# Near score tiles of a relative-position attention: one product kept from the row-maximum scan instead of two, with the row maximum taken off on ScalarE

## The chip, the cores and the metric

The kernel is one program on one NeuronCore of one Trainium2 chip. The time is device time in microseconds (us) of one execution, from launch to end on the core. A core has five instruction streams that run side by side and meet through semaphores: TensorE (PE; its weight loads, PEld, are a row of their own), VectorE (DVE), ScalarE (ACT), GpSimd (POOL) and SyncE (SP), the last mostly issuing DMAs. TensorE writes its products to PSUM, which here is eight banks of 128 partitions x 512 float32 numbers.

## The reference, cut to what matters

Two layers over x of shape (B, T, D) = (2, 1024, 128). Each computes, from one layer norm, an attention and a mixture of experts side by side, and adds both to x:

```
x = x + attention0(layernorm(x)) + experts0(layernorm(x))   # sigmoid attention, 32 experts of which 4 count
x = x + attention1(layernorm(x)) + experts1(layernorm(x))   # below;             16 experts of which 4 count
```

The change lies in the second attention and, in a small part, in the sorting for the second layer's experts. The second attention has 16 heads of 8 numbers and relative positions that are clipped at 128 on either side:

```
att_rel_pos = einsum('bhsd,pd->bhsp', q, pos_emb_k)          # 256 positions
att_idxs    = clip(key - query, -128, 127) % 256
att_pos     = att_rel_pos[:, :, query, att_idxs]
att         = softmax((q @ k^T + att_pos) / sqrt(8))          # over all 1024 keys, not causal
y           = (att @ v) @ Wproj^T
```

So only keys within 128 of the query have a position term that differs from key to key. Keys farther to the left all have the one term of position -128, keys farther to the right that of 127. In experts1, each of the 2048 tokens takes 4 of 16 experts; tokens are sorted by expert into blocks of 128 rows, moved there, run through their expert's three matrices, and moved back.

## The kernel before, in words

Stages, by the time of the profiled execution: up to 519 us the first layer's attention with its experts; 519 to 883 us the first half of the second attention; 883 to 1005 us the sorted expert blocks (experts, placed in the middle of the attention); from 1005 us the second half. The change touches the two stages of the second attention, and the last steps of the first stage, in which its pipeline is filled.

**Groups and steps.** The 16 heads are four sets s of four; the four heads of a set lie in the four bands of 32 partitions, so the four small matmuls of one operation lie in different rows of TensorE's array and partly overlap. T is cut into eight tiles of 128 and two halves q of 512. A group n = (b, s, q) is a batch, a set of heads and 512 queries: 16 groups. Each has eight steps, one for each tile kt of 128 keys: 128 steps. A pair of groups, q = 0 and q = 1 of the same heads, is the period of the work.

**Softmax in two passes.** Scores are held with keys on partitions and queries along the columns, so a row maximum can't be taken there. It is found ahead of time, from products that lie the other way round:

- by_position (L844) multiplies the queries by the 256 position vectors (less that of the far left) into four banks (L853); ACT copies them out (L857), DVE fills the third 128 columns with the last one (L859), and a DMA writes the rows to a buffer in DRAM with a row pitch W (L866). near_by (L870) reads them back with a pitch one shorter, which turns "column = relative position" into "column = key": the near tile of a query tile, [128 queries, 4 heads, 3 x 128 keys].
- scan(n, i, half) (L891) runs for query tile i of group n over four of the eight key tiles: four matmuls of 512 columns into four banks (L902). The keys kls and khs (operands, L834) carry the far-left or the far-right position already. On DVE the maxima of columns that need nothing more are plain reductions (L927). For the key tiles within one of the query tile, the near tile must be added first: one instruction adds, writes the sums to a scratch buffer, junk, and takes the maximum (L922). After the second half L930 takes the maximum over the pieces, negated, into negmax. Each of the eight scans of a group belongs to one step; they run LEAD = 10 steps ahead of the scores that need them.
- augment (L932) turns the four negmax tiles of a group (L937) and adds them to the queries as one more row (L941), called qa, against a row of ones in the keys: the product then is the score less its maximum.
- scores(n, kt) (L944) takes four banks, one for each head. A key tile within one of query tile i is "near": the near tile's part is transposed into the bank by a matmul with the identity (L953), head after head and within a head tile after tile, and the product of keys and qa (L963) is added on top of it over all 512 columns. In a group, three of the eight steps have no near tile, one has one, two have two and two have three: 11 near pairs, times four heads times 16 groups are 704 transposes. ACT takes the exponential from each bank to p (L970).
- values (L974) multiplies p by the values, one step later, into an accumulator bank (acc, L982); unload (L986, L994) takes it off after the group.

**What sets the order.** In this part PE's order is written by hand and kept: step t is scores(t), values(t - 1), scan(t + 10), with values split around the scan in some steps without near tiles; then, in two steps of a group, by_position and near_by for a later group, and in one step augment. After these come the pieces of work beside: the gate and sort1 in the early steps, later the moves of rows. The order on ACT, DVE, POOL and SP is set by the framework's scheduler from dependences and its own estimates of time, once, when the program is built; each engine then runs its list in that order.

**Banks.** Seven of the eight PSUM banks are one ring, "sm": each request takes the next one, the one given out seven requests before, and PE waits until its last reader is done. Scans, scores, position products, augment and sort1 all take from it. A step asks for eight banks (four for the scores, four for the scan), so it moves one on in the ring from step to step.

**sort1** (L535) counts, from the four choices of each token, where each token goes. Two products (L550, L551) go into one bank: rank, the number of tokens ahead in the same tile with the same expert, and in_tile, the count of each tile. in_tile is copied out, a running sum over the 16 tiles is built by 15 additions on DVE, and rank is read from the bank after these (L561).

Of the kernel before, what the change touches and what calls it, by code (L numbers as in the profile page):

```python
# [46 lines left out]
def fused_layers_kernel(ctx: ExitStack, tc: tile.TileContext, a: dict, out: bass.AP):  # L47
# [487 lines left out]
    def sort1():  # L535
# [13 lines left out]
        rank, in_tile = (ps[:, i * NTT * E1:(i + 1) * NTT * E1] for i in range(2))  # L549
        nc.tensor.matmul(rank, ahead, flat[0], start=True, stop=True)  # L550
        nc.tensor.matmul(in_tile, ones, flat[0], start=True, stop=True)  # L551
        rank, in_tile = (t.rearrange("p (t e) -> p t e", e=E1) for t in (rank, in_tile))
        nc.vector.tensor_copy(some, in_tile)
        nc.vector.memset(at[:, 0, :], 0.0)
        for t in range(1, NTT):
            if t % 8 == 1:
                yield
            nc.vector.tensor_add(at[:, t, :], at[:, t - 1, :], some[:, t - 1, :])
        nc.vector.tensor_add(n_tok, at[:, NTT - 1, :], some[:, NTT - 1, :])
        yield  # L560
        nc.vector.tensor_add(at, at, rank)  # L561
# [237 lines left out]
    def rows_of(r):  # L799
        return slice(32 * r, 32 * r + 32)  # L800
# [90 lines left out]
    def scan(n, i, half):  # L891

        b, s, q = groups[n]
        l1 = pools["l1"]
# [11 lines left out]
        if half == 0:  # L906
            maxima[n, i] = l1.tile([P, NG, 4], F32, tag="maxima", name="maxima", bufs=3), []
# [6 lines left out]
        for k0, k1, close in pieces:  # L914
            slot = len(used)
            used.append(slot)
            for r in range(NG):
                part = ps[r][:, (k0 - lo) * P:(k1 - lo) * P]
                if close:
                    junk = l1.tile([P, NEAR], F32, tag="junk", name="junk")  # L920
                    w0 = (k0 - (qt - 1)) * P
                    nc.vector.tensor_tensor_reduce(  # L922
                        junk[:, 0:(k1 - k0) * P], part, near[n, i][:, r, w0:w0 + (k1 - k0) * P],
                        1.0, -BIG, ALU.add, ALU.max, mx[:, r, slot:slot + 1],
# [3 lines left out]
        if half == 1:  # L928
            out_ = negmax[s, i].rearrange("p (r c) -> p r c", r=NG)[:, :, aux[s]]
            nc.vector.tensor_reduce(out_, mx[:, :, 0:len(used)], AX.X, ALU.max, negate=True)  # L930

# [12 lines left out]
    def scores(n, kt):  # L944
# [4 lines left out]
        close = [i for i in range(4) if abs(4 * q + i - kt) <= 1]  # L949
        for r in range(NG):  # L950
            for i in close:
                w0 = (kt - (4 * q + i) + 1) * P
                nc.tensor.matmul(  # L953
                    ps[r][:, i * P:(i + 1) * P], near[n, i][:, r, w0:w0 + P], ident,
                    is_transpose=True, start=(i == close[0]), stop=False, skip_group_check=True,
                )

        cut = min(max(kt - 1 - 4 * q, 0), 4)
# [326 lines left out]
```

## Time and profile before

| what | value |
|---|---|
| time, three runs | 1305.71, 1308.27, 1313.92 us; median 1308.27 |
| profiled execution | 1308.08 us; span from the first to the last instruction 1306.3 us |
| busy, of the span | TensorE 92%, VectorE 58%, ScalarE 48%, GpSimd 29% |
| mean granted TensorE clock | 0.966 of full speed |
| busy in 519 to 883 us (364 us) | PE 335.6, DVE 249.8, ACT 184.8, POOL 77.1 us |
| busy in 883 to 1005 us (122 us) | PE 114.7, DVE 64.6, ACT 50.6, POOL 0.0 us |
| busy in 1005 to 1306.3 us (301.3 us) | PE 278.0, DVE 184.2, ACT 155.9, POOL 145.3 us |

How to read its lines: "L953 PE MATMUL sm<-ident,near 128*128 128x128 f32 x704 | 108.4, 287 | 24.5 <-DVE maxima L927 11.3" is a group of instructions: those of line 953, matmuls into a bank "sm" from the identity and a near tile, 704 of them; they were busy for 108.4 us together, 287 ns each; before them PE stood idle for 24.5 us, of which 11.3 us were ended by DVE's maxima of line 927 (which read the bank that the transpose wanted). Matmuls overlap, so the length of one is more than the distance between two. In a timeline the first two numbers are the start and the length of a run of equal instructions in us, xN their number, and [1.41 <-PE sm L902] the idle time before the first of them with what ended it.

### The profile page before, as it was taken

Reading aid. Unit: us, or ns where it says so; the run is one execution under the profiler, and the core shown is the slowest. Engines: PE = TensorE matmul, PEld = TensorE weight load, DVE = VectorE, ACT = ScalarE, POOL = GpSimd, SP = SyncE. Lnnn points to the kernel's source line nnn. Section 1 sums busy time; section 2 is a strip of 40 time slices with the busy share of each in tenths; the row PEclk is TensorE's granted clock in tenths of the full one; section 3 lists DMA queues with packets and bytes.
Section 4 is the critical chain, followed back from the end, with each engine's and each line's share of the span. In section 5 each row is a group of like instructions: output and inputs, shape, how many; then the busy total and the mean of one; then the engine's idle time right before and its main releaser. Section 6 shows DMA issues by size and latency. Waiting matters only on the chain.

```text
span 1306.3 us, 23125 instructions
## 1 busy us (share of the span) xinstructions
PE 1197.7 (92%) x8567; PEld 566.9 (43%) x8567; DVE 759.4 (58%) x2178; ACT 625.0 (48%) x1102; POOL 378.2 (29%) x464
## 2 busy tenths in 40 slices
PE   5889999989999878899799999988999999998997
PEld 2323332333333333434344354448999444443433
DVE  7783333573322358776876756764555856666653
ACT  3634444535455342454355654543444555554463
POOL 1123243323323242001002444330000445446453
PEclk9889999989999989899899999998999999998998
DMA  6682212111111261344365644659997354663511
GB/s 181 175 229 85 59 57 57 33 33 49 41 49 41 82 217 61 126 147 145 98 194 178 201 142 161 218 185 278 293 293 228 110 171 157 208 215 115 181 47 29
DMA packets 146660, 181.77 MB, mean 139 GB/s; under 512 B 16436, under 2 KB 125236, under 8 KB 146292
## 3 DMA queue, kind: packets, MB, share of 16 engines
q1 hardware_dynamic: 142292, 171.37, 42.7%
q0 software_dynamic: 4256, 8.92, 2.4%
q8 instruction: 68, 1.11, 0.4%
q14 instruction: 44, 0.36, 0.1%
HBM read 110.81 MB, written 73.77 MB: 141 GB/s over the span
## 4 chain that ended last, share of the span: by engine, by line
PE 70%; DVE 17%; DMA 5%; ACT 4%; issue 2%; POOL 1%; SPq 0%; DVEq 0%; ACTq 0%; POOLq 0%
PE sm L963 11%; PE sm L902 9%; PE acc L982 8%; PE big L340 6%; PE sm L953 5%; PE big L449 5%; PE big L341 5%; PE acc L475 5%; PE ffn L367 4%; PE sm L704 4%; DVE junk L922 3%; PE sm L853 3%; DVE maxima L927 2%; PE sm L719 2%; DMA room<-wx 1%
## 5 line engine op out<-in xcount | busy, mean ns | idle before, releaser
L970 ACT ACTIVATE p<-sm 128x512 f32<-128x512 f32 x512 | 264.7, 607 | 234.1 <-PE sm L963 233.6
L927 DVE TENSOR_REDUCE maxima<-sm 128x1 f32<-128x512 f32 (+3 forms) x472 | 226.7, 502 | 99.2 <-PE sm L902 99.2
L455 ACT ACTIVATE at<-big 128x1024 f32<-128x1024 f32 (+1 forms) x192 | 144.9, 808 | 149.7 <-PE big L449 143.7
L922 DVE CUSTOM_DVE_ANT_0 junk<-sm,near 128x384 f32<-128x384 f32 (+2 forms) x292 | 130.3, 446 | 66.3 <-PE sm L902 66.3
L982 PE MATMUL acc<-p,vs 128*32 128x512 f32 (+1 forms) x1288 | 146.4, 524 | 0.4 <-ACT yu L994 0.4
L352 DVE SCALAR_TENSOR_TENSOR t<-big,b,sg 128x512 f32<-128x512 f32 x64 | 47.9, 749 | 158.0 <-ACT sg L351 158.0
L355 POOL TENSOR_TENSOR h<-h,cb 128x512 f32<-128x512 f32 x64 | 82.8, 1294 | 195.5 <-DVE h L353 185.3
L953 PE MATMUL sm<-ident,near 128*128 128x128 f32 x704 | 108.4, 287 | 24.5 <-DVE maxima L927 11.3
L902 PE MATMUL sm<-kls,qs 32*128 32x512 f32 (+2 forms) x776 | 107.5, 580 | 6.2 <-POOL kls L834 5.0
L963 PE MATMUL sm<-qa,kls 32*128 32x512 f32 (+3 forms) x832 | 112.9, 560 | 0.0
L630 POOL DMA_INDIRECT got<-slots_y,slot_of x64 | 65.1, 1017 | 164.6 <-ACT p L970 152.5
L953 PEld LDWEIGHTS sm<-ident,near 128*128 128x128 f32 x704 | 78.0, 143 | 79.2 <-ACT p L970 35.4
L449 PE MATMUL big<-qm,xT 32*128 32x512 f32 (+3 forms) x768 | 103.8, 555 | 1.3 <-DVE xT L249 0.6
L618 POOL DMA_INDIRECT slots_x<-xn,slot_of x64 | 62.8, 981 | 95.8 <-ACT p L970 86.3
L475 PE MATMUL acc<-at,xn 128*32 128x512 f32 (+3 forms) x768 | 84.8, 514 | 5.9 <-POOL at L460 4.0
L340 PE MATMUL big<-xT,w 128*128 128x512 f32 x128 | 74.5, 665 | 14.9 <-DVE h L353 12.5
L857 ACT COPY rel<-sm 128x512 f32<-128x512 f32 x112 | 57.5, 600 | 61.6 <-PE sm L853 61.6
L640 POOL TENSOR_SCALAR got<-got,share 128x128 f32<-128x128 f32 x64 | 41.1, 642 | 110.1 <-DMA got<-slots_y,slot_of 110.0
L367 PE MATMUL ffn<-h,w 128*128 128x512 f32 x128 | 72.8, 651 | 0.0
L982 PEld LDWEIGHTS acc<-p,vs 128*32 128x32 f32 x1288 | 26.6, 109 | 105.9 <-issue 95.4
L902 PEld LDWEIGHTS sm<-kls,qs 32*128 32x128 f32 x776 | 36.9, 186 | 81.1 <-ACT p L970 21.1
L460 POOL TENSOR_SCALAR_AFFINE_SELECT at<-at 128x512 f32<-128x512 f32 x64 | 41.5, 648 | 101.6 <-ACT at L455 101.2
(285 smaller groups left out, 1659.8 us busy)
## 6 DMA issues: line engine op xcount, KB each, us to landing
bounce<-rel SPq DMA_DIRECT2D x64, 768.0 KB
near<-bounce SPq DMA_DIRECT2D x64, 768.0 KB
cb<-cw SPq DMA_DIRECT2D x128, 128.0 KB
blockw<-wx SPq DMA_DIRECT2D x53, 304.0 KB
room<-wx SPq DMA_DIRECT2D x26, 304.0 KB
slots_x<-zeros SPq DMA_DIRECT2D x19, 256.0 KB
slots_y<-by SPq DMA_DIRECT2D x19, 256.0 KB
room<-slots_x SPq DMA_DIRECT2D x17, 256.0 KB
```

Of the source, the lines that this page charges most:

```text
L340: nc.tensor.matmul(hh[0:m, 0, :], wa, xT, start=True, stop=True)
L367: nc.tensor.matmul(y, w2m, h[0:m], start=first, stop=last and bias_mm is None)
L449: nc.tensor.matmul(halves[r // 2][:, r % 2, off:TB], xT0[b][g, kt * P:(kt + 1) * P], masked[b, s][g, q * TB + off:(q + 1) * TB], start=Tru ...
L455: nc.scalar.activation(at[:, 2 * j:2 * j + 2, off:TB], sc[:, :, off:TB], AF.Sigmoid, scale=4.0 / math.sqrt(HD))
L475: nc.tensor.matmul(y[32 * r:32 * r + 32, off:TB], xn0[b][:, kt * P + 32 * r:kt * P + 32 * r + 32], at[:, r, off:TB], start=(kt == 0), stop ...
L902: nc.tensor.matmul(ps[r][:, (k0 - lo) * P:(k1 - lo) * P], qs[g, qt * P:(qt + 1) * P], (kh if far else kl)[g, k0 * P:k1 * P], start=True, s ...
L922: nc.vector.tensor_tensor_reduce(junk[:, 0:(k1 - k0) * P], part, near[n, i][:, r, w0:w0 + (k1 - k0) * P], 1.0, -BIG, ALU.add, ALU.max, mx[ ...
L927: nc.vector.tensor_reduce(mx[:, r, slot:slot + 1], part, AX.X, ALU.max)
L953: nc.tensor.matmul(ps[r][:, i * P:(i + 1) * P], near[n, i][:, r, w0:w0 + P], ident, is_transpose=True, start=(i == close[0]), stop=False, ...
L963: nc.tensor.matmul(ps[r][:, i0 * P:i1 * P], k[g, kt * P:(kt + 1) * P], qa[n][g, i0 * P:i1 * P], start=(m == 0 and not close), stop=(m == l ...
L970: e = nc.scalar.activation(p[:, r, :], ps[r], AF.Exp)
L982: nc.tensor.matmul(y[rows_of(r), part], vs[:, kt, rows_of(r)], probs[n, kt][:, r, part], start=(kt == 0), stop=(kt == NT - 1 and part.stop ...
```

## The change

**Near tiles.** The in-place sum replaces junk: in the scan the instruction that adds the near tile and takes the maximum now writes its sums, the finished scores, back into the near tile. A new function, take_off, adds negmax to these columns on ScalarE (one activation Identity with a bias column for each head; 384 columns, or 256 for the first and last query tile). In scores, the near tiles are transposed as before, but nothing is added to them: the product with qa covers only the columns that aren't near, those left of the near tiles (c0) with khs and those right of them (c1) with kls. The transposes now run tile after tile, and within a tile head after head.

**Order of the scans.** For q = 0, a group now scans the far half of the keys (key tiles 4 to 7) for its four query tiles first, then the near half for the four (tile_of); for q = 1 the order is as before. So up to six tiles of maxima are open, and L930's counterpart runs after the half that holds the last piece (half == q). In the written order of the program take_off stands after scores(t): for heads 0 and 1 two steps after the scan that finished the tile, for heads 2 and 3 three steps after.

**sort1.** Both products are copied out of the bank at once; the running sum is built in place, and rank is added at the end from the copy.

```diff
--- before.py
+++ after.py
@@ -546,19 +546,17 @@
         yield
         nc.vector.tensor_add(some, some, chosen[3])
         ps = small()
-        rank, in_tile = (ps[:, i * NTT * E1:(i + 1) * NTT * E1] for i in range(2))
-        nc.tensor.matmul(rank, ahead, flat[0], start=True, stop=True)
-        nc.tensor.matmul(in_tile, ones, flat[0], start=True, stop=True)
-        rank, in_tile = (t.rearrange("p (t e) -> p t e", e=E1) for t in (rank, in_tile))
-        nc.vector.tensor_copy(some, in_tile)
-        nc.vector.memset(at[:, 0, :], 0.0)
+        for i, m in enumerate((ahead, ones)):
+            nc.tensor.matmul(ps[:, i * NTT * E1:(i + 1) * NTT * E1], m, flat[0], start=True, stop=True)
+        nc.vector.tensor_copy(flat[1], ps[:, 0:NTT * E1])
+        nc.vector.tensor_copy(flat[0], ps[:, NTT * E1:2 * NTT * E1])
         for t in range(1, NTT):
             if t % 8 == 1:
                 yield
-            nc.vector.tensor_add(at[:, t, :], at[:, t - 1, :], some[:, t - 1, :])
-        nc.vector.tensor_add(n_tok, at[:, NTT - 1, :], some[:, NTT - 1, :])
+            nc.vector.tensor_add(some[:, t, :], some[:, t, :], some[:, t - 1, :])
+        nc.vector.tensor_copy(n_tok, some[:, NTT - 1, :])
         yield
-        nc.vector.tensor_add(at, at, rank)
+        nc.vector.tensor_add(at[:, 1:, :], at[:, 1:, :], some[:, 0:NTT - 1, :])
         by_e = [P, E1, E1]
         nc.vector.tensor_tensor(some, spread(n_tok, NTT), filled.unsqueeze(1).to_broadcast(by_e), ALU.is_gt)
         nc.vector.tensor_reduce(n_blk, some, AX.X, ALU.add)
@@ -888,9 +886,15 @@
 
     maxima = {}
 
-    def scan(n, i, half):
+    def tile_of(n, m):
+
+
+        return (m // 2, m % 2) if groups[n][2] else (m % 4, 1 - m // 4)
+
+    def scan(n, m):
 
         b, s, q = groups[n]
+        i, half = tile_of(n, m)
         l1 = pools["l1"]
         qs, kl, kh, _ = head[b, s]
         qt = 4 * q + i
@@ -903,8 +907,8 @@
                     ps[r][:, (k0 - lo) * P:(k1 - lo) * P], qs[g, qt * P:(qt + 1) * P],
                     (kh if far else kl)[g, k0 * P:k1 * P], start=True, stop=True,
                 )
-        if half == 0:
-            maxima[n, i] = l1.tile([P, NG, 4], F32, tag="maxima", name="maxima", bufs=3), []
+        if (n, i) not in maxima:
+            maxima[n, i] = l1.tile([P, NG, 4], F32, tag="maxima", name="maxima", bufs=6), []
         mx, used = maxima[n, i]
         n0, n1 = max(lo, qt - 1), min(hi, qt + 2)
         if n0 >= n1:
@@ -917,17 +921,27 @@
             for r in range(NG):
                 part = ps[r][:, (k0 - lo) * P:(k1 - lo) * P]
                 if close:
-                    junk = l1.tile([P, NEAR], F32, tag="junk", name="junk")
+
                     w0 = (k0 - (qt - 1)) * P
+                    whole_ = near[n, i][:, r, w0:w0 + (k1 - k0) * P]
                     nc.vector.tensor_tensor_reduce(
-                        junk[:, 0:(k1 - k0) * P], part, near[n, i][:, r, w0:w0 + (k1 - k0) * P],
-                        1.0, -BIG, ALU.add, ALU.max, mx[:, r, slot:slot + 1],
+                        whole_, part, whole_, 1.0, -BIG, ALU.add, ALU.max, mx[:, r, slot:slot + 1],
                     )
                 else:
                     nc.vector.tensor_reduce(mx[:, r, slot:slot + 1], part, AX.X, ALU.max)
-        if half == 1:
+        if half == q:
             out_ = negmax[s, i].rearrange("p (r c) -> p r c", r=NG)[:, :, aux[s]]
             nc.vector.tensor_reduce(out_, mx[:, :, 0:len(used)], AX.X, ALU.max, negate=True)
+
+    def take_off(n, i, heads):
+
+        b, s, q = groups[n]
+        qt = 4 * q + i
+        w0, w1 = (max(qt - 1, 0) - (qt - 1)) * P, (min(qt + 2, NT) - (qt - 1)) * P
+        for r in heads:
+            t = near[n, i][:, r, w0:w1]
+            c = 32 * r + aux[s]
+            nc.scalar.activation(t, t, AF.Identity, bias=negmax[s, i][:, c:c + 1])
 
     def augment(n):
 
@@ -946,24 +960,23 @@
         b, s, q = groups[n]
         _, kl, kh, _ = head[b, s]
         ps = [small() for _ in range(NG)]
-        close = [i for i in range(4) if abs(4 * q + i - kt) <= 1]
-        for r in range(NG):
-            for i in close:
-                w0 = (kt - (4 * q + i) + 1) * P
+        c0, c1 = (min(max(kt + d - 4 * q, 0), 4) for d in (-1, 2))
+        for i in range(c0, c1):
+            w0 = (kt - (4 * q + i) + 1) * P
+            for r in range(NG):
                 nc.tensor.matmul(
                     ps[r][:, i * P:(i + 1) * P], near[n, i][:, r, w0:w0 + P], ident,
-                    is_transpose=True, start=(i == close[0]), stop=False, skip_group_check=True,
+                    is_transpose=True, start=True, stop=True,
                 )
 
-        cut = min(max(kt - 1 - 4 * q, 0), 4)
-        parts = [(0, cut, kh)] * (cut > 0) + [(cut, 4, kl)] * (cut < 4)
-        for m, (i0, i1, k) in enumerate(parts):
+        for i0, i1, k in ((0, c0, kh), (c1, 4, kl)):
             for r in range(NG):
-                g = rows_of(r)
-                nc.tensor.matmul(
-                    ps[r][:, i0 * P:i1 * P], k[g, kt * P:(kt + 1) * P], qa[n][g, i0 * P:i1 * P],
-                    start=(m == 0 and not close), stop=(m == len(parts) - 1), skip_group_check=True,
-                )
+                if i0 < i1:
+                    g = rows_of(r)
+                    nc.tensor.matmul(
+                        ps[r][:, i0 * P:i1 * P], k[g, kt * P:(kt + 1) * P], qa[n][g, i0 * P:i1 * P],
+                        start=True, stop=True,
+                    )
         p = pools["late"].tile([P, NG * TB], F32, tag="p", name="p", bufs=2)
         p = p.rearrange("p (r c) -> p r c", r=NG)
         for r in range(NG):
@@ -1100,7 +1113,9 @@
     at(N_ATT + 8, turned1, 1)
     at(N_ATT + 9, blocks1, 1)
     for m in range(LEAD):
-        at(N_ATT + 8 + m, scan, m // 8, m % 8 // 2, m % 2)
+        at(N_ATT + 8 + m, scan, m // 8, m % 8)
+        if 4 <= m < 8:
+            at(N_ATT + 9 + m, take_off, 0, m - 4, range(NG))
     at(N_ATT + 10, by_position, 1, 1)
     at(N_ATT + 13, queries, 0, 1)
     at(N_ATT + 13, operands, 0, 1)
@@ -1197,6 +1212,12 @@
             if t < N_STEPS:
                 scores(t // 8, t % 8)
 
+            for back in (2, 3):
+                m = t + LEAD - back
+                n, k = m // 8, m % 8
+                if LEAD - 2 <= m < N_STEPS and (k % 2 if groups[n][2] else k >= 4):
+                    take_off(n, tile_of(n, k)[0], range(2 * back - 4, 2 * back - 2))
+
 
             n, kt = (t - 1) // 8, (t - 1) % 8
             halved = 0 < kt and t != EXPERTS and t + 1 < N_STEPS and not is_near(t + 1) and not before
@@ -1204,7 +1225,7 @@
                 values(n, kt, left if halved else whole)
             m = t + LEAD
             if m < N_STEPS:
-                scan(m // 8, m % 8 // 2, m % 2)
+                scan(m // 8, m % 8)
             if halved:
                 values(n, kt, right)
             for f, args in before:
```

## The prediction

> **What bounds the kernel now.** I read the page's busy shares first, then windows by stage, then the groups by shape, then the timeline of single steps.
>
> ```profile
> PE 1197.7 (92%) x8567; PEld 566.9 (43%) x8567; DVE 759.4 (58%) x2178; ACT 625.0 (48%) x1102; POOL 378.2 (29%) x464
> ```
> ```profile
> 1056.40:1133.10 76.70, 74.14 (x657) 34.33 (x658) 51.78 (x167) 42.22 (x83) 38.81 (x53) 1.00 0.57 180
> ```
> TensorE is the busiest engine overall. The second line is one undisturbed pair of groups (16 of the 128 steps; columns: length, then busy time of PE, weight loads, DVE, ACT and POOL, clock, DMA). PE is busy 74.1 of 76.7 us, so what PE waits for decides. I call steps 0.0 to 0.7 those of the even group (q = 0) and 1.0 to 1.7 those of the odd one; the pair starts at step 0.0.
>
> ```profile
> 1123.25 1.14 PE L902 MATMUL sm<-kls,qs 32*128 32x512 f32 x8
> 1124.32 0.55 PE L953 MATMUL sm<-ident,near 128*128 128x128 f32 x3
> 1125.32 0.30 PE L953 MATMUL sm<-ident,near 128*128 128x128 f32 x1 [0.45 <-DVE maxima L922]
> 1125.55 1.14 PE L963 MATMUL sm<-qa,kls 32*128 32x512 f32 x8
> ...
> 1131.95 1.14 PE L902 MATMUL sm<-kls,qs 32*128 32x512 f32 x8
> 1133.03 1.53 PE L953 MATMUL sm<-ident,near 128*128 128x128 f32 x12
> 1134.48 1.14 PE L963 MATMUL sm<-qa,kls 32*128 32x512 f32 x8
> ```
> Step 1.3 (one near tile): scan, three transposes, then 0.45 us idle until DVE has freed the fourth bank, one transpose, product. Step 1.5 (three tiles): twelve transposes and no wait. The scan takes four of seven banks, the scores the next four: heads 0 to 2 get the banks of the previous exps 1 to 3, head 3 the first bank that DVE gives back from the scan just done. With heads outside, three tiles hide that wait behind nine transposes.
>
> ```profile
> 1124.41 0.29 DVE L927 TENSOR_REDUCE maxima<-sm 128x1 f32<-128x128 f32 x1 [1.41 <-PE sm L902]
> 1124.62 0.55 DVE L922 CUSTOM_DVE_ANT_0 junk<-sm,near 128x384 f32<-128x384 f32 x1
> 1125.09 0.08 DVE L922 DVE_READ_ACCUMULATOR2_ANT maxima<- 128x1 f32 x1
> ```
> DVE starts when the scan ends, frees a bank each 0.68 us (1124.41 to 1125.09), and with L930 has the tile's maximum 3.0 us after that start.
>
> ```profile
> L970 ACT ACTIVATE p<-sm 128x512 f32<-128x512 f32 x512 | 264.7, 607 | 234.1 <-PE sm L963 233.6
> L351 ACT ACTIVATE sg<-big,b 128x512 f32<-128x512 f32 x64 | 44.0, 687 | 49.8 <-PE big L341 49.5
> L963 PE MATMUL sm<-qa,kls 32*128 32x512 f32 x512 | 86.1, 656 | 0.0
> ```
> ACT waits for PE before its exps and not the other way round. Four exps take 2.06 us in the timeline, just what PE needs (values 1.0, scan 1.07) before it asks for their banks.
>
> ```profile
> 620.73 0.73 PE L853 MATMUL sm<-posd,qs 32*128 32x256 f32 x6 [1.36 <-DVE at L561]
> 626.73 2.07 PE L853 MATMUL sm<-posd,qs 32*128 32x256 f32 x10 [5.26 <-DVE maxima L927]
> ```
> The sort: 1.36 us are the bank held until L561, 5.26 us are DVE busy with the sort itself.
>
> **What the Trainium skill says.** "ScalarE: Activation LUTs", What ACT_TABLE_LOAD costs: an ACTIVATE with immediates takes 186 ns + 0.833 ns per column, each pointer operand adds about 93, and following ones overlap by 93. The trace agrees: 607 for 512 columns against 612, and 687 with a bias column against 705. The same page, Table sets: identity is in every set, so no table load comes in; no Identity runs in the kernel before. "PSUM — Partial Sum Buffer", Engine vs sequencer instructions: ScalarE and VectorE queues are strict FIFO. "TensorE: Matmul & The Clock Gate", What's actually happening: an idle window of about 3.4 us halves the clock; in the sort the granted clock falls to 0.63 and 0.50, after the 5.26 us wait.
>
> **The change, part by part** (per pair).
>
> (1) Product columns that go. The start-to-start distance of a product is 1.07 us for 512 columns, 0.75 for 384, 0.54 for 256, 0.33 for 128. Before, each of 16 steps costs 1.07: 17.2. After, even group 0.54, 0.33, 0.33, 0.54, 0.75, 3 x 1.07; odd 3 x 1.07, 0.75, 0.54, 0.33, 0.33, 0.54: 11.4. That is -5.7 of PE time. The 44 transposes stay.
>
> (2) Transposes with tiles outside and heads inside (scores). PE now asks for the fourth bank after three transposes in every near step, so it waits as in step 1.3, and the rest of the transposes (0.122 us each) come after the wait: four more in a 2-tile step (+0.49, against 0.53 saved), while in a 3-tile step the product starts 1.00 + 0.23 + 8 x 0.122 = 2.2 after the first transpose instead of 1.45 (+0.73, against 0.74 saved). Four steps of each kind: +4.9. (1) and (2) together leave -0.8, nearly all from the two 1-tile steps.
>
> (3) DVE order. The built order of the changed kernel has, in two scans per pair (steps 0.1 and 1.3), the sums of all four heads ahead of the plain maxima of all four, so that the first bank comes back after 2.1 us and not 0.7: +1.4 each. Step 1.4 pays it in full. At 0.1 the position products (L853) pay it, but before's own wait there (0.6 us at 1078.70, and 0.17 in 0.2) goes: net +0.6. Together +2.0. The in-place write itself is as wide as the junk write and costs nothing; DVE's maxima order over the halves moves work between steps and adds none.
>
> (4) ScalarE. 256 new activations, 192 of 384 columns and 64 of 256: 600 and 493 ns by the page (bias is a pointer), 0.51 and 0.40 back to back; some 147 us busy, so per pair 42.2 + 18 of 77 and no bound by itself. The trace bounds it from below: 0.40 and 0.29 without the bias column. What decides is the place. PE alone has its order written by hand; ACT's built order puts the first take-off of a tile not two steps after its scan but ahead of the very next step's exps, in all pairs alike: scan 0.3 before exps 0.4, 0.5 before 0.6, 1.3 before 1.4, 1.4 before 1.5, 1.5 before 1.6. ACT then stands until DVE has that scan's maximum, 3.1 us after the scan's end, and four exps wait behind it, PE's next banks behind these.
> Step 0.4: scores end 1.9 after scan 0.3; the take-off ends at 3.1 + 0.6 = 3.7; exps 1.8 late. Head 3 of the scan waits 1.05, the next scores 0.5: +1.5. Step 0.6: exps 2.0 late, and one take-off of 0.4 stands between each two of them, so the fourth ends 3.2 late; the position products need it with 0.8 in hand: +2.4. Step 1.5: exps 1.6 late: +1.1; 1.6: +0.8 at the position products; take-offs behind the rel copies in 0.1: +0.4. Sum 6.2, less what steps 1.7 and the next 0.0 give back because their bank waits overlap with it (1.2) and about 0.5 that the 0.2 us pauses of the halved steps take up: +4.5, or +2.7 with the shorter activations.
>
> (5) Sort. The bank goes at once, -1.3 at most; two copies (0.42 each) replace one copy and a memset, and the DVE run of 9.5 us ahead of the maxima gets some 2 us shorter while the same work comes later. I take -1.3.
>
> (6) Even groups scan the far half first, so the fourth tile's near sums are wanted three steps after their positions, not four. Rows leave at 668.39 and are back at 676.4 in the SP timeline: 8 us against three steps of over 4: hidden; were it not, 1 us a pair. Six maxima buffers and the missing junk cost nothing.
>
> **Sum.** Per pair -5.7 + 4.9 + 2.0 + 4.5 = +5.7. Six pairs: +34.2. The pair with the sort hides its first terms behind it: +4.5. The last pair has no scans in its last ten steps: +3.9 from steps 0.4 and 0.6, and there the columns do count (-2.9): +1.0. Sort -1.3. Together +38.4. The profiled execution took 1308.08 us (span 1306.3 and 1.8 around it), the median of the runs 1308.27: the forecast is 1346 us. With the shorter activations it is 1333, with every give-back missing 1358: its own range is 1330 to 1362.
>
> **Rivals.** A: ACT's waits are hidden, because the exps have more slack than I read; then -0.8 + 2.0 a pair stays, +9 less 1.3 and 2.9: 1313. For it: ACT idles 234 us before the exps. Against it: this idle time lies before the scores, not after them. B, the other side: the fourth bank. If it is free when PE asks (DVE frees it 0.35 us sooner than in step 1.3, since nothing else is queued), waits (2) to (4) shrink and the columns count: -5.7 x 8 is -45, with a third of it lost to exps some -30: 1278. It decides once the bank is back within 0.6 us of the first transpose; before, it is 1.0. C: the PE pauses at L853 grow past 3.4 us, the clock halves once a pair as in the sort: 3 us more each: 1370. For it: the two waits there are over 2 us.
>
> **How the numbers follow.** Forecast 0.57, A 0.16, B 0.18, C 0.09. The range leaves out most of B and of C: 1290 to 1365. A tells from no change only by over 1% (13 us), about what this measurement can tell: slower 0.57 + 0.09 and no part of A, 0.66; within 1% 0.16; faster 0.18.
>
> **What would show it.** (1) L963's counterpart loses a third of its busy time. (2) three transposes, a pause of about 0.45 ended by DVE maxima, then the others, in 2- and 3-tile steps. (3) a pause near 1.9 in step 1.4. (4) take-offs waiting for DVE negmax, exps starting over 1.5 us after the scores' end, and a PE pause at the position products of 0.6 ended by ACT p. (5) the wait for L561 gone, 5 us on DVE maxima left. The forecast is wrong if ACT's exps still start within 0.1 us of the scores.

## The result, and the profile after

The changed kernel takes 1383.78 us (median of 4 runs, 1375.78 to 1387.33), the kernel before 1306.99 us beside it: a ratio of 1.057, 95% interval 1.0508 to 1.0632. It is slower by 77 us, where 38 were forecast (1346 us, with 1290 to 1365 as the range). The profiled execution took 1384.05 us, with a span of 1382.3 us and a mean granted clock of 0.934 (before: 0.966). Below, a run that lay over 1.5% above the fastest of its kernel is left out of ratios and means (one each of E11 and E13).

The page's busy shares come first:

```profile
PE 1236.5 (89%) x8247; PEld 578.1 (42%) x8247; DVE 754.1 (55%) x2178; ACT 745.7 (54%) x1358; POOL 377.9 (27%) x464
```

TensorE issues 320 matmuls fewer, and yet it is busy for 39 us more: its matmuls run at a lower clock. Its idle time (span less busy) grew too, from 108.6 to 145.8 us. The next lines are the two rows of PE's waits that changed most, and the row of DVE's that is new (total us, times, longest):

```profile
PE sm L851 <- DVE maxima L931: 39.5, 14, 6.1
PE sm L967 <- DVE maxima L931: 19.4, 32, 1.6
```
```profile
DVE near L927 <- DMA near<-bounce: 24.2, 7, 5.6
```

L851 are the position products (L853 before). Their wait for DVE is 39.5 us now; the same row of the trace before has 9.4:

```profile
PE sm L853 <- DVE maxima L927: 9.4, 15, 5.3
```

In 7 cases DVE itself stood still, because the near tile it was to add hadn't come back from DRAM. No such row stood in the trace of before.

The groups of ScalarE, by shape:

```profile
L983 ACT ACTIVATE p<-sm 128x512 f32<-128x512 f32 x512 | 268.3, 603 | 115.9 <-PE sm L976 115.0
L944 ACT ACTIVATE near<-near,negmax 128x384 f32<-128x384 f32 x192 | 110.0, 624 | 77.1 <-DVE negmax L934 77.0
L944 ACT ACTIVATE near<-near,negmax 128x256 f32<-128x256 f32 x64 | 30.3, 510 | 25.9 <-DVE negmax L934 25.9
```

Before, ScalarE idled 234.1 us ahead of its exps, for PE. Now 103 us of its idle time lie ahead of the take-offs (77.1 + 25.9), for the maximum that they take off, with exps queued behind them.

**One pair, step by step.** The same pair of groups in both traces, from the scores of step 1.1 to those of the next 1.1 (1038.57 to 1115.13 us before, 1081.35 to 1171.20 us after). Each number is the time from the first matmul of a step's scores to that of the next step's, in us:

| step | 1.1 | 1.2 | 1.3 | 1.4 | 1.5 | 1.6 | 1.7 | 0.0 | 0.1 | 0.2 | 0.3 | 0.4 | 0.5 | 0.6 | 0.7 | 1.0 | sum |
|---|---|---|---|---|---|---|---|---|---|---|---|---|---|---|---|---|---|
| before | 4.73 | 4.32 | 4.37 | 4.34 | 4.61 | 7.12 | 4.43 | 4.42 | 7.39 | 5.03 | 4.34 | 4.72 | 3.48 | 5.92 | 3.65 | 3.69 | 76.6 |
| after | 9.43 | 6.20 | 4.12 | 5.75 | 5.81 | 6.67 | 4.11 | 4.32 | 8.68 | 5.96 | 4.24 | 5.89 | 3.61 | 7.88 | 3.50 | 3.68 | 89.9 |
| more | 4.7 | 1.9 | -0.3 | 1.4 | 1.2 | -0.5 | -0.3 | -0.1 | 1.3 | 0.9 | -0.1 | 1.2 | 0.1 | 2.0 | -0.2 | 0.0 | 13.3 |

More than half of the 13.3 us lies in three steps (1.1, 1.2 and 0.2) that the forecast had at nothing or little. PE's timeline of step 1.1, and the windows around it (columns as in the prediction, with the number of instructions behind each busy time; the last three are the clock, the DMA share and GB/s):

```profile
1084.47 0.85 PE L851 MATMUL sm<-posd,qs 32*128 32x256 f32 x6
1089.77 1.64 PE L851 MATMUL sm<-posd,qs 32*128 32x256 f32 x9 [4.45 <-DVE maxima L931]
```
```profile
1084.50:1089.00 4.50, 0.82 (x10) 0.42 (x4) 0.06 (x1) 0.07 (x1) 2.81 (x5) 1.00 0.70 236
1089.00:1096.50 7.50, 6.74 (x38) 3.17 (x42) 3.50 (x14) 4.03 (x8) 4.47 (x6) 0.54 0.31 106
1096.50:1103.00 6.50, 4.99 (x51) 2.16 (x43) 4.78 (x20) 3.64 (x8) 2.75 (x5) 1.00 0.97 284
```

PE stands still for 4.45 us, then its clock is halved for 7 us, which makes step 1.2 longer by 1.9; the same after the pause of step 0.1 (3.4 us at half clock from 1137.2 us) makes 0.9 in step 0.2. What DVE waits for in step 1.1 is seen one pair later in the chain of waits (start, length, what):

```profile
1165.22 0.77 DVE rel L857 x2
...
1166.09 6.64 DMA bounce<-rel
...
1172.78 7.11 DMA near<-bounce
...
1180.02 0.29 DVE near L927
```

The rows of the pair's first tile leave at 1165.67 us, those of the second at 1166.09. The second tile's are 6.6 us on the way to DRAM and 7.1 us on the way back. DVE is ready for this tile at 1174.4 us, 5.6 us before it starts on it.

Most of the other steps are near the forecast (not step 1.6, which is 0.5 us shorter where 0.8 more were forecast). Step 1.4, where DVE does the sums of all four heads first:

```profile
1101.10 0.91 PE L967 MATMUL sm<-ident,near 128*128 128x128 f32 x3
1103.44 0.77 PE L967 MATMUL sm<-ident,near 128*128 128x128 f32 x5 [1.44 <-DVE maxima L931]
```

And ScalarE in step 0.6, where the take-offs of a tile stand ahead of and between the exps:

```profile
1158.68 0.51 ACT L944 ACTIVATE near<-near,negmax 128x256 f32<-128x256 f32 x1 [2.91 <-DVE negmax L934]
1159.09 0.58 ACT L983 ACTIVATE p<-sm 128x512 f32<-128x512 f32 x1
1159.57 0.50 ACT L944 ACTIVATE near<-near,negmax 128x256 f32<-128x256 f32 x1
1159.97 0.58 ACT L983 ACTIVATE p<-sm 128x512 f32<-128x512 f32 x1
```

### The profile page after: what moved, and what is told of

It is laid out like the page before. It is cut to its first block, busy times and chain, and to the rows that moved or that the text cites. A ratio compares the mean times of both kernels' runs of the same rounds, so it can differ in the third digit from the quotient of the medians.

```text
span 1382.3 us, 22668 instructions
## 1 busy us (share of the span) xinstructions
PE 1236.5 (89%) x8247; PEld 578.1 (42%) x8247; DVE 754.1 (55%) x2178; ACT 745.7 (54%) x1358; POOL 377.9 (27%) x464
## 3 DMA queue, kind: packets, MB, share of 16 engines
q1 hardware_dynamic: 142292, 171.37, 39.5%
## 4 chain that ended last, share of the span: by engine, by line
PE 61%; DVE 21%; DMA 8%; ACT 6%; issue 3%; POOL 1%; SPq 0%; DVEq 0%; ACTq 0%; POOLq 0%
PE sm L906 8%; PE acc L995 8%; PE sm L976 6%; PE sm L967 6%; PE big L340 5%; DVE near L927 5%; DVE maxima L931 5%; PE big L449 5%; PE big L341 4%; PE acc L475 4%; PE ffn L367 4%; PE sm L702 4%; DMA near<-bounce 3%; DMA bounce<-rel 2%; ACT p L983 2%
## 5 line engine op out<-in xcount | busy, mean ns | idle before, releaser
L931 DVE TENSOR_REDUCE maxima<-sm 128x1 f32<-128x512 f32 (+3 forms) x472 | 220.8, 501 | 150.8 <-PE sm L906 150.8
L944 ACT ACTIVATE near<-near,negmax 128x384 f32<-128x384 f32 (+1 forms) x256 | 140.3, 596 | 102.9 <-DVE negmax L934 102.9
L927 DVE CUSTOM_DVE_ANT_0 near<-sm,near 128x384 f32<-128x384 f32 (+2 forms) x292 | 124.7, 446 | 80.5 <-PE sm L906 56.3
L995 PE MATMUL acc<-p,vs 128*32 128x512 f32 (+1 forms) x1288 | 158.7, 564 | 0.7 <-ACT yu L1007 0.6
L967 PE MATMUL sm<-ident,near 128*128 128x128 f32 x704 | 119.5, 302 | 34.3 <-DVE maxima L931 19.4
L906 PE MATMUL sm<-kls,qs 32*128 32x512 f32 (+2 forms) x776 | 133.2, 601 | 3.6 <-ACT p L983 1.3
L967 PEld LDWEIGHTS sm<-ident,near 128*128 128x128 f32 x704 | 85.0, 151 | 89.3 <-ACT p L983 28.4
L851 PE MATMUL sm<-posd,qs 32*128 32x256 f32 x448 | 69.6, 461 | 41.5 <-DVE maxima L931 39.5
L906 PEld LDWEIGHTS sm<-kls,qs 32*128 32x128 f32 x776 | 45.5, 197 | 105.1 <-ACT p L983 42.5
L976 PE MATMUL sm<-qa,kls 32*128 32x512 f32 (+3 forms) x512 | 73.3, 563 | 0.0
```

The source lines that it names most:

```text
L906: nc.tensor.matmul(ps[r][:, (k0 - lo) * P:(k1 - lo) * P], qs[g, qt * P:(qt + 1) * P], (kh if far else kl)[g, k0 * P:k1 * P], start=True, s ...
L927: nc.vector.tensor_tensor_reduce(whole_, part, whole_, 1.0, -BIG, ALU.add, ALU.max, mx[:, r, slot:slot + 1],)
L931: nc.vector.tensor_reduce(mx[:, r, slot:slot + 1], part, AX.X, ALU.max)
L944: nc.scalar.activation(t, t, AF.Identity, bias=negmax[s, i][:, c:c + 1])
L967: nc.tensor.matmul(ps[r][:, i * P:(i + 1) * P], near[n, i][:, r, w0:w0 + P], ident, is_transpose=True, start=True, stop=True,)
L976: nc.tensor.matmul(ps[r][:, i0 * P:i1 * P], k[g, kt * P:(kt + 1) * P], qa[n][g, i0 * P:i1 * P], start=True, stop=True,)
```

## The experiments

After the result I held this theory (L): four things add up in the changed kernel. The near tile lands too late for the scan of step 1.1; the take-offs hold up exps; DVE's order holds up a bank; the order of the transposes shows a wait. The half clock comes behind the pauses that these make. The rivals: (A) ScalarE's places are the root, and the landing is late only because the exps of step 0.6 are; (B) the ring of banks bounds, so that each wait that goes lets the next one appear; (C) the half clock has a price of its own.

Ratios are to the kernel before, run beside each on the same chip; they can differ by up to 0.4% from the quotient of two medians (E1: 1.0479, where 1369.03/1301.16 is 1.0522). By the intervals, a difference between two of the ratios is good to some 8 to 13 us. Half clock is counted in each profiled execution from 519 us to 12 us before the end, in windows of half a microsecond: 44 us in the kernel before, 140 in the changed one (149 with the end). This is one execution each: by the mean clocks of 39 executions of the kernel before, counted over the whole span, half clock varied from 60 to 87 us, so that small differences of it say nothing.

**E1: the far half of the fourth query tile later.**

```diff
     def tile_of(n, m):
-        return (m // 2, m % 2) if groups[n][2] else (m % 4, 1 - m // 4)
+        first = ((0, 1), (1, 1), (2, 1), (0, 0), (1, 0), (2, 0), (3, 1), (3, 0))
+        return (m // 2, m % 2) if groups[n][2] else first[m]
...
-                if LEAD - 2 <= m < N_STEPS and (k % 2 if groups[n][2] else k >= 4):
+                if LEAD - 2 <= m < N_STEPS and (k % 2 if groups[n][2] else k in (3, 4, 5, 7)):
```

> The changed kernel, with one thing moved: for q = 0 the far half of the fourth query tile is scanned as seventh of eight scans, not as fourth, so that the first sums with the second pair of near tiles come two steps later. Theory L (the near tiles land too late, and the pause at the position products of step 1.1 halves the clock behind it): DVE's waits for near tiles, 24.2 us in 7, fall under 5; PE's waits at the position products, 40.5 us, fall under 20; some 50 of the 149 us at half clock go. The time falls by 24 + 0.5 x 50 less some that is lost again: 1383.8 to about 1340. Theory A (ScalarE's places are what counts, and the landing only takes a place among other waits): at most -12 us, 1372 or more.

Measured: 1369.03 us, ratio 1.0479 (1.0402 to 1.0555), against 1.057: about -12 us, as theory A had it, though the two intervals overlap and this much alone isn't clear of the scatter. But the landing did go: DVE has no wait for near tiles any more, and PE's waits at the position products fell to 19.2 us (17.1 for DVE, 2.1 for ScalarE). Half clock hardly fell, to 130 us. ScalarE's timeline tells why:

```profile
1078.37 2.07 ACT L984 ACTIVATE p<-sm 128x512 f32<-128x512 f32 x4 [0.44 <-PE sm L977]
1083.56 0.51 ACT L945 ACTIVATE near<-near,negmax 128x256 f32<-128x256 f32 x1 [3.12 <-DVE negmax L935]
1083.97 2.02 ACT L855 COPY rel<-sm 128x512 f32<-128x512 f32 x4
1085.87 0.63 ACT L984 ACTIVATE p<-sm 128x512 f32<-128x512 f32 x1
```

Moving the scans makes the scan of step 1.1 the one that finishes a tile, so its take-off now stands ahead of the copies and the exps of the next step: a new stop of 3.1 us where the landing was. ScalarE's idle time ahead of take-offs rose from 103 to 131.5 us. The edit alone doesn't price the landing.

**E2: take-offs behind the exps.**

```diff
-            nc.scalar.activation(t, t, AF.Identity, bias=negmax[s, i][:, c:c + 1])
+            a_ = nc.scalar.activation(t, t, AF.Identity, bias=negmax[s, i][:, c:c + 1])
+            if "name" in last_exp:
+                tc.add_manual_dep(a_.ins, last_exp["name"], mybir.DependencyInfo(
+                    mybir.DependencyClass.NoSync, mybir.DependencyReason.SCHED_ONLY), reason="pace")
```

> The changed kernel, with each take-off queued on ScalarE behind the exps that stand before it in the program, so that it comes two and three steps after its scan, as written. Theory L: the exps of steps 0.4, 0.6 and 1.5 are on time, 1.2 + 2.0 + 1.2 us a pair come back, 4.4 x 8 = 35; the position products of step 0.6 come 2 us sooner and so does the landing, which then costs some 2 us and not 4 a pair; with some of the half clock gone too about -55, to 1329, with DVE still waiting for near tiles by 5 to 15 us. Theory A: the late exps are the root of the landing's lateness and of the clock, DVE's waits for near tiles go entirely and the time comes to 1310 or less. If the places are hidden: no change.

Measured: 1344.26 us, ratio 1.0322 (1.0287 to 1.0357): -32 us. DVE's waits for near tiles did not go, they grew to 31.0 us in 7 cases; half clock is 130 us. Theory A falls: with the exps on time the near tile is still late, since the scan that wants it comes sooner too. The gain is near the 35 us that the late exps themselves were to cost, without the further gain that theory L hoped for.

**E3: transposes with heads outside, as before.**

```diff
-        for i in range(c0, c1):
-            w0 = (kt - (4 * q + i) + 1) * P
-            for r in range(NG):
+        for r in range(NG):
+            for i in range(c0, c1):
+                w0 = (kt - (4 * q + i) + 1) * P
```

> The changed kernel, with the transposes in the order of before: heads outside, tiles inside. By step (2) of the prediction the wait for the fourth bank is then hidden behind two or three tiles of three heads: 4.9 us a pair less, 8 x 4.9 = 39, and PE's waits at the transposes fall from 34 us to under 15. Rival: the wait moves to the product or to the scan and little comes back, 0 to -10 us. Half clock and landing stay as they are.

Measured: 1366.12 us, ratio 1.0492 (1.0456 to 1.0527): -10 us. The waits at the transposes for DVE fell from 30.7 to 18.2 us, while the scan's waits for ScalarE rose from 1.7 to 6.0 us. PE's idle time in all hardly moved (143.7 us against 145.8). The rival of this expectation holds: little comes back, and most of what is hidden here seems to be waited for elsewhere. The 10 us are just clear of the scatter.

**E4: sums and maxima head after head.**

```diff
-        for k0, k1, close in pieces:
-            slot = len(used)
-            used.append(slot)
-            for r in range(NG):
+        slots = range(len(used), len(used) + len(pieces))
+        used.extend(slots)
+        for r in range(NG):
+            for slot, (k0, k1, close) in zip(slots, pieces):
```

> The changed kernel, with the sums and maxima of a scan written head after head and not piece after piece, so that in no scan do the sums of all four heads stand before the maxima that free the first bank. By step (3) of the prediction: 2 us a pair, -14 to -16 us, and the wait of 1.44 us at the transposes of step 1.4 falls to about 0.4. Rival: DVE stands still for the landing or for PE in these steps, and the order makes no difference (within 5 us).

Measured: 1354.88 us, ratio 1.0401 (1.0368 to 1.0434): -22 us, more than step (3) put on it. The waits at the transposes for DVE are 20.5 us and none of those for L931 is longer than 1.3 us. The position products' wait for DVE fell too, from 39.5 to 30.3 us, though the landing stayed (25.1 us in 7). The two together are 19.4 us less. Half clock fell to 96 us, the most by any single edit.

**E5: the four together.** The four diffs above.

> The changed kernel with the four edits of the runs so far together: far half of the fourth tile later, take-offs behind the exps, transposes with heads outside, sums head after head. Alone they gave ratios to the kernel before of 1.048, 1.032, 1.049 and 1.040 against 1.057 without: -12, -33, -10 and -22 us. Theory W (each takes away its own wait, and the half clock is the consequence of the waits): they add up or better, half clock comes back to about the 44 us of before, and the product columns that are gone begin to count: ratio 0.965 to 1.00 (1256 to 1301 us). Theory B (the banks' ring is what bounds, and a wait that goes lets the next one appear): ratio 1.02 or more.

Measured: 1270.43 us, ratio 0.9744 (0.969 to 0.9799). It beats both kernels: 34 us less than the kernel before. Together the edits took away 108 us, where alone they took 76. That is what theory W of this expectation forecast, and against theory B. Half clock is 41 us, as before the change. PE idles as long as in the kernel before (110.3 us against 108.6) and is busy for 36.5 us less (1161.2 us); its products with qa alone are busy for 38.9 us less (127.1 us against 166.0). So the 34 us are about what the columns that are gone had cost. One rival stays: the order of the sums was not tried alone in the kernel before, and may have a part in them. ScalarE in steps with take-offs:

```profile
1073.18 1.14 ACT L945 ACTIVATE near<-near,negmax 128x384 f32<-128x384 f32 x2
1074.69 2.06 ACT L987 ACTIVATE p<-sm 128x512 f32<-128x512 f32 x4 [0.37 <-PE sm L980]
1076.61 1.14 ACT L945 ACTIVATE near<-near,negmax 128x384 f32<-128x384 f32 x2
1078.48 2.05 ACT L855 COPY rel<-sm 128x512 f32<-128x512 f32 x4 [0.73 <-PE sm L851]
```

The take-offs are as many and as long as before these edits (136 us, 605 ns each), and ScalarE waits 0.2 us ahead of them in all, instead of 103. A pair takes 72.7 us (from one unload of an accumulator to the next but one, 1014.05 to 1086.75 us), 3.9 less than in the kernel before.

**E6: the pause of step 1.1 filled, in the changed kernel.**

```diff
+            fill = [0, 1, 2] * 4 if q and j == pair == 0 and "sm" in psum else []
-            for r in range(NG):
+            for r in [0, 1, 2] + fill + [3]:
```

> The changed kernel, with twelve position products of heads 0 to 2 done again, to the same result, ahead of the one that waits, at step 1.1 of each pair: 24 passes of some 0.13 us, 3 us of work that lies in the pause of 2 to 6 us. It adds TensorE work and takes no wait away. Theory C (the half clock behind a pause has a price of its own): half clock behind these pauses falls by 5 us or more in each of 7 pairs, half of which is time, and the kernel gets faster by 10 to 20 us although it does more. If the clock's fall is only a sign of waits and costs nothing: no change, or slower by as much as a pause is shorter than its filling.

Measured: 1384.25 us, ratio 1.0625 (1.0566 to 1.0683): no gain. The run is inconclusive. A pass took 0.07 us and not 0.13, so the filling was 1.7 us long and pauses of 1 to 2.8 us stayed; half clock fell all the same, to 106 us in the profiled execution, the shortest of five, and by the mean clocks of all runs from 165 to 145 us. A better filling is E13.

**E7: the kernel before, with a near tile later.**

```diff
-            at_step(8 * n - 15 + 5 * pair, positions, n, pair)
+            at_step(8 * n - 15 + (5 if q else 6) * pair, positions, n, pair)
```

> The kernel before, with the second position products of even groups one step later (step 0.7 and not 0.6), so that their near tiles have three steps until they are wanted, as in the changed kernel. Theory L: rows are away for 14 us (6.6 written, 7.1 read back), the pause of 2 to 6 us at step 1.1 or 1.2 appears, with half clock behind it: +25 to +50 us. By step (6) of the prediction (8 us away, hidden): within 5 us.

Measured: 1302.17 us, ratio 0.9989 (0.997 to 1.0009): nothing, against theory L. So three steps are enough there. SP's issues of the DMAs, and DVE's first work on the near tile:

```profile
1111.98 0.91 SPq L866 DMA_DIRECT2D bounce<-rel  x2
1116.25 3.51 SPq L877 DMA_DIRECT2D near<-bounce  x2
```
```profile
1123.29 0.29 DVE L927 TENSOR_REDUCE maxima<-sm 128x1 f32<-128x128 f32 x1 [0.98 <-PE sm L902]
1123.49 0.55 DVE L922 CUSTOM_DVE_ANT_0 junk<-sm,near 128x384 f32<-128x384 f32 x1
```

In this order the first tile of the pair is wanted first, 11.5 us after the rows left (1111.98 to 1123.49). By the DMAs' semaphores in the trace it was back 9.7 us after they left, and the second tile 11.9 us after. The changed kernel wants the second tile first, and sooner: in its seven cases 8.2 to 11.1 us after the rows left, while the first tile was back after 9.5 to 12.2 us and the second after 12.0 to 14.2. So both count: which tile is wanted first (the second comes 2.0 to 3.6 us after the first), and how many microseconds three steps last from the rows' leaving. Had the first tile been the one wanted, at the same moments, DVE would still have waited in three of the seven cases, by these times.

**E8: the sort alone, in the kernel before.** The diff of sort1 above.

> The kernel before, with the edit of sort1 alone. By step (5) of the prediction -1.3 us: the wait for L561 goes, the 5 us on the maxima stay. Rival: with the bank free the pause only moves to the maxima, and nothing changes.

Measured: 1305.78 us, ratio 1.0019 (0.9998 to 1.0041): no gain. PE's wait for L561 is gone, and the longest wait for the maxima at the position products is now 7.0 us instead of 5.3. The rival holds: the pause only changed its name.

**E9 to E12: the four together, less one each.**

> The four edits together (ratio to before 0.974) without the first: the far half of the fourth tile is scanned fourth again. Theory L: DVE waits for near tiles again, 20 to 31 us in 7, PE stands at the position products, half clock grows from 41 us by 24 to 48: +25 to +50 us, ratio 0.995 to 1.015. Theory A (with the exps on time the landing is in time): within 8 us, ratio under 0.982.

> The four edits together without the second: the take-offs stand on ScalarE where the scheduler put them, ahead of the next step's exps. By step (4) of the prediction +4.5 us a pair, in all +31 to +36 us, with half clock behind the position products of step 0.6 another +10: ratio 1.00 to 1.01. If the place of the take-offs mattered only together with late landings: within 10 us, ratio under 0.983.

> The four edits together without the third: sums and maxima of a scan written piece after piece. By step (3) of the prediction +2 us a pair, +14 to +16 us, ratio 0.985. By the single edit, which gave -22 us: +22, ratio 0.99. If the waits for the first bank lie beside others: within 5 us.

> The four edits together without the fourth: transposes with tiles outside and heads inside, as in the changed kernel. By step (2) of the prediction +4.9 us a pair: +35 to +39 us, ratio 1.00, with PE's waits at the transposes back from 12 to over 30 us. By the single edit, which gave -10 us: +10, ratio 0.982.

| edit | alone on the changed kernel (1.057) | change | left out of the four (0.9744) | change |
|---|---|---|---|---|
| far half of the fourth tile later | 1.0479 (E1) | -12 us | 1.0038, 1.001 to 1.0066 (E9) | +38 us |
| take-offs behind the exps | 1.0322 (E2) | -32 us | 1.0256, 1.0212 to 1.03 (E10) | +67 us |
| sums head after head | 1.0401 (E4) | -22 us | 0.9933, 0.9914 to 0.9951 (E11) | +25 us |
| transposes with heads outside | 1.0492 (E3) | -10 us | 0.9847, 0.9807 to 0.9886 (E12) | +13 us |

The changes are differences of ratios times 1307; by the intervals each is good to some 8 to 9 us, E1's to 13. Medians of E9 to E12: 1310.91, 1337.10, 1298.36 and 1286.35 us. E9 prices the landing, in the kernel with the other three edits: DVE waits for near tiles again, and half clock is 82 us instead of 41.

```profile
DVE near L927 <- DMA near<-bounce: 30.3, 7, 4.9
```

Theory L's number (+25 to +50) holds, and theory A is out for good, since in E9 ScalarE doesn't wait ahead of its take-offs at all. In E10 ScalarE waits 78 us for negmax ahead of the take-offs, and the stop at step 1.1, which the changed kernel doesn't have, is there: its 67 us are more than the take-offs cost in the changed kernel. E11 and E12 came out as the single edits did. That the right column adds up to 143 us, and the whole is 108, says that the costs overlap; a reading that fits is that where two of them hold up the same step, each alone is enough.

**E13: E9 with its pauses filled.** As E6, with `[0, 1, 2] * 8`.

> The three edits without the far half moved (ratio 1.004, whose seven pauses for a landing are 3.9 to 4.6 us each and are followed by 6.8 to 10.2 us at half clock), with 24 position products of heads 0 to 2 done again ahead of the one that waits: 48 passes of 0.07 us, 3.5 us of work inside each pause. It does more and waits for the same landing. Theory C (half clock has a price of its own): the half clock behind these pauses, some 50 us in all, goes, half of it is time: -20 to -25 us, ratio 0.985 to 0.99. Rival (half clock behind a pause costs nothing, since other waits take it up): within 5 us, ratio 1.00 or more.

Measured: 1302.96 us, ratio 0.9974 (0.9944 to 1.0003), against 1.0038 without the filling: -8 us although it does 168 products (336 passes) more. The waits left in the seven pauses are 0.4 to 1.3 us. By the mean clock of all the runs compared, E9 spends 120 us at half clock and E13 78 us (twice one minus the clock, times the span), with mean times of 1310.6 and 1300.6 us: 10 us for 42 us of half clock, 0.24 us for each (0.13 to 0.35 by the scatter of the runs). Theory C's sign holds, at about half its size. That waits which are there anyway take up the rest is a guess; no run shows it.

## Why the prediction was wrong

- **The side was right, the size was half.** Of the 13.3 us of a pair, 5.8 are left without steps 1.1, 1.2 and 0.2 (13.3 - 4.7 - 1.9 - 0.9). The sum of the prediction was 5.7. What failed in the main lies in these three steps. That the rest agrees so closely is partly luck: step 1.6 came out 1.3 us below its forecast, and steps 1.7 and 0.0 gave back 0.4 us where 1.2 were to come.
- **Step (6) failed: the landing, which it put at nothing.** It compared 8 us of absence with "three steps of over 4", and both sides were wrong. "Rows leave at 668.39 and are back at 676.4 in the SP timeline" read a row of SP's queue as a transfer. The row at 672.83 with a length of 3.53 us ends when the second read-back is *issued*. By the DMAs' semaphores in that same trace the two tiles were back at 678.22 and 681.58 us, the second 13.2 us after the rows left; in the changed kernel it was 12.0 to 14.2. "Perfetto Trace Analysis" of the Trainium skill says just this (DMA Instruction — HWDGE: the row of the issuing engine leaves out the data movement). The other side, the three steps, was 8.2 to 11.1 us and not over 12: steps 0.7 and 1.0 last only some 3.6 us each, and the rows leave when step 0.7 has begun. The step also didn't ask which of a pair's two tiles is wanted first; it was the one that comes back last. So the bound "were it not, 1 us a pair" was too low as well: PE stood for 4.45 us in the pair shown, and by E9 against E5 the landing costs 38 us in all with the half clock behind it. This price is of the kernel with the other repairs; in the changed kernel itself E1 put another stop in its place.
- **Rival C was right in kind.** It was given 9 in 100: the pauses at the position products grow and the clock halves once a pair, 3 us each on top of the forecast. It didn't name what would make them grow. By the page's clocks there are 182 us at half clock (2 x 0.066 x 1382.3) against 89 before (2 x 0.034 x 1306.3), 93 us more. At E13's 0.24 this is an estimate of 22 us. The 24.2 us of waits for the landing and these 22, on top of the 38 forecast, come to 84, against 77 measured; the two may overlap.
- **(1) and (2), columns against transposes:** near enough in the changed kernel. Steps 1.3, 1.7, 0.0 and 0.3 are within 0.3 us of before, 0.8 less together, with the pause after three transposes where it was put. The products were to lose a third of their busy time; they lost 14% in the changed kernel (166.0 to 142.8 us, in part at half clock) and 23% in E5 (127.1 us). One figure of (2) was summed a little low: by its own terms +0.73 is 0.76, 0.1 us a pair. But undoing (2) doesn't give 39 us back; E3 and E12 give 10 and 13. The pauses were where the term put them; as a price of the edit it was too high by a factor of three or more.
- **(3), DVE's order:** step 1.4 costs 1.4, as said, with a pause of 1.44 us where one near 1.9 was named as a sign. In the whole kernel it is worth 22 to 25 us (E4, E11) and not 16. E4's waits of PE that went are 10.2 us at the transposes and 9.2 at the position products; half clock fell with them, and what of the rest is its share isn't shown.
- **(4), ScalarE's places:** 1.2, 2.0 and 1.2 us in steps 0.4, 0.6 and 1.5, against 1.5, 2.4 and 1.1; in 1.6 the 0.8 didn't show (-0.5). The durations were right (0.51 and 0.40 us back to back). The PE pause of 0.6 us at the position products of step 0.6 shows only as two of 0.19 us. E2 gives 32 us back, against 8 x 4.5 = 36, so rival A (these waits are hidden) is out.
- **(5), the sort:** -1.3 forecast, nothing measured (E8).
- **Rival B** was out in the changed kernel. E5 comes near it: with the waits gone a pair takes 3.9 us less than before, and the kernel 34 us less in all, where B had some 30.

## What to carry to other kernels

In these traces a row of the queue that issues DMAs ends with the issue (1173.14 us in the pair shown, where the tile landed at 1179.89). How long data is away is read from the chain of waits or from who waits for it, for the transfer that is wanted first, and compared with microseconds, not with steps. An operation written "two steps later" in the program was put elsewhere by the scheduler, on an engine whose order isn't pinned; once the take-offs were pinned behind the work that they must not hold up, ScalarE waited 0.2 us ahead of the same 256 activations instead of 103. When several waits hold up the same step, undo all of them before judging an idea: here each repair alone gave 10 to 32 us, and the four together turned +77 into -34.

## What the runs showed that I had not expected

- Half clock came in stretches of 3.4, 6.8 and 10.2 us, in two kernels also of 13.7, but for the last stretch of each execution. In the changed kernel it followed pauses of 2.3 us (676.0 to 678.3 us) and less: one stretch of 6.8 us began at 754.9 us with only 0.4 us of idle time in the records of the 7 us before it, while position products waited bank by bank for exps. The window of about 3.4 us that the Trainium skill gives ("TensorE: Matmul & The Clock Gate", What's actually happening) is seen in these lengths; but a pause need not fill it for the clock to fall.
- A microsecond at half clock cost 0.24 us here (E9 against E13, 0.13 to 0.35), not 0.5.
- Each near tile is one transfer of 768 KB each way. In the pair shown the second tile's took 6.6 us to DRAM and 7.1 us back, beside the first tile's and other traffic.
